# Two-layer spectral attention over 56 planes: the mix of images made once and kept, in three of four passes

## The chip, the cores and the metric

The kernel runs on one NeuronCore of a Trainium2 chip. Its five engines are TensorE (PE: matrix products; PEld stands for its weight loads), VectorE (DVE), ScalarE (ACT), GpSimd (POOL) and SyncE (SP, which issues the DMAs). The metric is the device time of one execution in microseconds, in fp32 throughout. A profile is one execution recorded by the hardware profiler; its span is the time from the first to the last recorded instruction.

## The reference

The input x holds 2 images (b = 0, 1), each of K = 56 planes of 128 x 128. Two layers follow each other, each of the form x = x + conv(gn(x)). Cut to what matters here:

```python
for layer in (0, 1):
    xa = gn(x)                               # one plane each: B*K planes of one channel
    q, k, v = (fno(inorm(xa)) for 3 sets)    # 1 channel -> 8 heads
    out  = softmax(q k^T / 128) v            # over the 56 planes, per head
    att  = inorm(fno_P(out) + xa)            # 8 heads -> 1 channel
    h    = gelu(inorm(spectral_M0(inorm(att))) + skip_M0(inorm(att)))
    h    = inorm(spectral_M1(h)) + skip_M1(h)
    x    = x + inorm(h) + att
```

Here `fno` is a spectral convolution (rfft2, a product on 2 x 16 x 16 modes, irfft2) plus a skip of 1 x 1. All skips are linear in the planes, so everything of `att` that is not confined to the few kept modes is one 56 x 56 matrix applied to the planes of the image: the "mix of images". It enters the forward path twice in a layer, each time times one factor per plane: once below the gelu, and once in the residual at the end.

## The kernel before, in words

One pass is one image in one layer; the kernel makes four: pass 0 and 1 are layer 0 with b = 0 and 1, pass 2 and 3 layer 1. The image stands in SBUF as X2 (partitions: 56 planes twice over, upper and lower rows of a chunk; row 56 of each half is a row of constants), and everything else of a pass happens in the space of modes. The stages of a pass and the names used for them are single letters, which are also tokens of the order of work:

- t (turn): PE transposes the image in 8 pieces, ACT copies them to P (L420); k: DVE's bn_stats of the planes (L426); m, n: forward transform; g, c: gram matrix of the modes for the norms.
- q (`scale_x`, L610): POOL multiplies X2 in place by the factor gvr of each row, in 8 pieces of 1024 columns; after the last a DMA puts gvr itself in row 56 of X2.
- u, s, v, a, d: scores, values, softmax and heads, from which the matrix BTx of the mix comes.
- p (`norms_chain`, from L773): the norms. From sums over the modes it makes three factors per plane, spread out as w; it transforms the low modes back halfway (`inverse`), and then makes two scaled copies of the matrix, Bs = BTx * w0 and Be = BTx * w2.
- y (`gelu`): for each of 8 slots of 1024 columns, PE puts the synthesis of the low modes in a PSUM pair (`synthesis`, L828, 16 matmuls for a slot), adds the mix of X2 with Bs (`mixed`, L843, 4 matmuls of 512 columns for a slot), and ACT takes the gelu of that PSUM pair to P (L859). `h3(b, n)` is slot n of P.
- z (`gelu_stats`, L866): DVE's bn_stats of the gelu's output, two for a slot. b (`turn_back`): PE transposes the slots (L409), ACT copies them out (L876). f (`forward`, L893): PE's transform back to modes. h (`h_chain`): the second spectral layer and its norms on these modes, ending in the factor hs (L957).
- x (`end_x`): loads of the residual x into xr, which has three slots of 1024 columns, by SP's DMAs; in pass 3 POOL restores it from X2 instead (`from_x2`, L981).
- e (`end_sums`): per slot again a synthesis, and again the mix of X2, now with Be; in pass 3 also xr, by a matmul (L1007).
- o (`end_out`): DVE makes h * hs + the PSUM pair (L1018), POOL adds xr (L1021, not in pass 3), and SP stores: to `out` in layer 1, to a DRAM buffer in pass 0. Layer 0 leaves the new x in X2.
- W, R, A, B, C, O prepare the weights, mostly on POOL.

The order of work is written out by hand as one string of tokens, ORDER: each token is a letter with the number of the pass, and advances that pass's generator by one step. Every engine executes its instructions in exactly this order (`_in_order`); between engines a tile framework sets the semaphores. So one instruction that has to wait holds back all that follow on its engine. PSUM has two rotating banks (`bank`) and three rotating pairs of banks (`pair`), given out in the order of the calls.

Of the kernel before, what the change touches and what calls it, by code (L numbers as in the profile page):

```python
# [37 lines left out]
F32 = mybir.dt.float32  # L38
# [105 lines left out]
t0 t0 t0 t0 W0 t0 t0 t0 x0 k0 k0 k0 k0 k0 k0 k0 t0 k0 m0 m0 m0 n0 m0 n0 m0 m0 W0 W0 W0 t1 W0 k1 n0 m0 m0 n0 n0 t1 t1  # L144
t1 g0 g0 g0 g0 k1 k1 k1 g0 R0 g0 n0 q0 q0 t1 t1 t1 t1 R0 R0 k1 k1 k1 R0 k1 m1 R0 A0 A0 A0 g0 g0 c0 c0 m1 u0 u0 m1 n1
m1 m1 n1 n1 c0 m1 n1 m1 n1 n1 u0 u0 u0 s0 g1 g1 g1 W1 W1 m1 g1 g1 g1 g1 g1 c1 A0 s0 s0 c1 u0 u0 u0 c1 u1 u1 W1 u1 s1
u1 u1 B0 B0 B0 s0 s0 x0 s1 s1 u1 u1 u1 s0 a0 s1 s1 v1 v0 v0 a0 v0 B0 s1 a1 v0 v0 a0 W1 W1 R1 d0 d0 d0 d0 a0 v1 a0 p0
v1 a1 q0 C0 p0 p0 p0 v1 v1 O0 p0 q0 q0 q0 q0 q0 a1 d1 d1 p0 p0 p0 a1 p0 d1 d1 q1 a1 p1 R1 q1 p1 p1 p1 y0 y0 z0 y0 R1
R1 R1 z0 b0 b0 p1 R1 y0 C0 R1 y0 y0 f0 f0 f0 b0 q1 q1 z0 z0 x0 q1 q1 q1 y0 y0 y0 p1 p1 b0 f0 b0 p1 p1 f0 b0 f0 z0 z0
y0 y0 y0 f0 f0 q1 b0 y1 f0 z0 z0 b0 y1 f0 f0 f0 y1 y1 y1 y1 b1 b1 h0 h0 h0 h0 h0 h0 z1 z1 y1 y1 y1 y1 z1 z1 z1 z1 y1  # L150
h0 f1 f1 f1 z1 y1 z1 b1 b1 h0 h0 f1 b1 f1 b1 f1 h0 f1 f1 b1 f1 h0 h0 b1 f1 f1 f1 h1 h0 e0 e0 o0 e0 x0 h1 o0 x0 e0 e0
t2 e0 e0 e0 o0 h1 h1 h1 h1 e0 e0 x0 o0 x0 e0 e0 o0 x0 t2 o0 o0 x1 k2 h1 k2 t2 o0 h1 h1 h1 k2 t2 k2 h1 t2 k2 h1 t2 t2
t2 e1 A1 h1 O1 e1 k2 k2 k2 x1 x1 e1 e1 e1 o1 x1 e1 o1 m2 o1 m2 e1 e1 e1 t3 t3 x1 o1 o1 x1 x1 x1 o1 k3 m2 m2 m2 m2 m2
t3 t3 k3 e1 e1 n2 n2 o1 x2 n2 n2 e1 o1 x2 t3 m2 t3 g2 g2 g2 g2 A1 A1 k3 k3 k3 k3 t3 t3 g2 g2 g2 g2 k3 c2 n2 n2 k3 m3
m3 c2 B1 C1 u2 u2 m3 n3 m3 m3 m3 m3 n3 n3 c2 u2 n3 n3 n3 q3 q3 u2 u2 m3 g3 g3 g3 g3 A1 g3 s2 g3 g3 g3 s3 s2 s2 c3 u2
u2 u2 u3 u3 u3 u3 c3 s2 s2 s2 B1 B1 B1 s3 s3 a2 v2 v2 u3 u3 u3 u3 a2 v2 v2 q2 q2 q2 a2 q2 q2 q2 q2 s3 s3 c3 C1 v2 s3
a3 d2 d2 d2 d2 a2 v3 a2 p2 a3 v3 p2 p2 p2 v3 v3 v3 p2 a3 d3 d3 q3 q3 q3 q3 p2 p2 p2 a3 p2 d3 d3 a3 y2 q2 y2 y2 p3 p3
p3 p3 b2 b2 p3 z2 f2 y2 y2 y2 p3 b2 f2 b2 z2 f2 p3 y2 y2 y2 z2 z2 p3 p3 f2 f2 b2 y2 b2 y2 y2 z2 z2 z2 z2 q3 f2 f2 f2
f2 q3 b2 y3 b2 y3 x2 z3 y3 z3 f2 f2 f2 b3 y3 b3 y3 y3 h2 h2 h2 h2 f3 f3 f3 y3 y3 y3 z3 h2 z3 z3 h2 b3 b3 h2 z3 f3 f3
f3 b3 b3 h2 h2 y3 y3 f3 h2 y3 b3 h2 h2 h2 f3 f3 b3 f3 f3 e2 e2 f3 e2 e2 e2 e2 e2 h3 o2 x2 o2 x2 o2 x2 h3 h3 h3 z3 o2  # L160
x2 z3 h3 e2 h3 h3 x3 e2 o2 x2 h3 h3 e2 e2 e2 o2 h3 o2 h3 h3 h3 x3 o2 x3 x3 e3 e3 o3 e3 e3 e3 x3 e3 x3 x3 x3 e3 e3 e3
e3 e3 o3 o3 x3 o3 o3 o3 o3 e3 o3
# [19 lines left out]
def fno_layers(ctx: ExitStack, tc: tile.TileContext, x, out, weights, small, const):  # L182
# [9 lines left out]
    ps = pool("psum", 2, space=bass.MemoryType.PSUM)  # L192
    pq = pool("pair", 3, space=bass.MemoryType.PSUM)
    dp = pool("dram", 1, space=bass.MemoryType.DRAM)

    def bank():
        return ps.tile([N, 512], F32, name="bank")

    def pair():
        return pq.tile([N, 2, 512], F32, name="pair")  # L200

    def little(name, shape):
        return sm.tile(shape, F32, name=name)
# [38 lines left out]
    V.memset(eps, EPS)  # L242
    ones = cp.tile([K, N], F32, name="ones")
# [16 lines left out]
    def padded(name, rows, m, n):  # L260
# [6 lines left out]
    xf_, gc_, BT_, Bs_, Be_ = (  # L267
        padded(*a) for a in (("xf", N, 448, 456), ("gc", K, K, 64), ("BT", K, K, 64), ("Bs", N, K, 64), ("Be", N, K, 64))
    )
# [336 lines left out]
    def scale_x(L, b):  # L606
        gvr = st[L][b]["gvr"]
        for o in range(0, 64, 8):
            v = X2[:120, b, o : o + 8, :]
            G.tensor_tensor(v, v, _bc(gvr[:120], 1, 8), ALU.mult)  # L610
            if o == 56:
                for c in range(2):
                    k = 64 * c + K
                    Q.dma_start(out=X2[k : k + 1, b], in_=_bc(gvr[k : k + 1, :], 1, 64))
            yield
# [157 lines left out]
    def norms_chain(L, b):  # L773
# [26 lines left out]
        V.reciprocal(k3, k3)  # L800
        yield
        w = rows([k3[:, 1:2], k3[:, 2:3], k3[:, 0:1]], [over[:, 1], over[:, 2], over[:, 0]])
        p = pair()
        t, dc, dq = p[:, 0, :448], p[0:1, 1, :K], p[0:1, 1, K : 2 * K]
# [12 lines left out]
        V.tensor_tensor(Bs_[b][:, :K], s["BTx"][:, :K], w[:, 0, :], ALU.mult)  # L817
        yield

        V.tensor_tensor(Be_[b][:, :K], s["BTx"][:, :K], w[:, 2, :], ALU.mult)  # L820
# [3 lines left out]
    def synthesis(A, both, Z):  # L824
        for e in range(4):
            for j in range(4):
                o = 64 * (8 * A + 2 * e)
                T.matmul(  # L828
                    both[j // 2][:, j % 2, N * e : N * e + N], lhsT=Z[32 * j : 32 * j + 32, o : o + N],
                    rhs=C["gw"][32 * j : 32 * j + 32, :], start=(e == 0), stop=False, tile_position=(32 * j, 0),  # L830
                    skip_group_check=True,
                )

    def mixed(L, b, A, v, p, Bs, stop=True):

        for c in range(2):
            s = 16 * A + (8 * v + 4 * c if L == 0 else 8 * c + 4 * v)  # L840
            for r in range(2):
                q = slice(64 * r, 64 * r + K + 1)
                T.matmul(  # L843
                    p[64 * c : 64 * c + 64, r, :], lhsT=Bs[q, :], rhs=X2[q, b, s : s + 4, :].rearrange("p e w -> p (e w)"),
                    start=False, stop=stop, tile_position=(64 * r, 64 * c), skip_group_check=True,
                )

    def h3(b, n):
        return P[b][:, 1024 * n : 1024 * n + 1024]

    def gelu(L, b):
        s = st[L][b]
        for A in range(4):
            both = [pair(), pair()]
            synthesis(A, both, s["Z"])
            yield
            for v in range(2):
                mixed(L, b, A, v, both[v], Bs_[b])
                S.activation(h3(b, 2 * A + v), both[v].rearrange("p r m -> p (r m)"), AF.Gelu)  # L859
                yield  # L860

    def gelu_stats(L, b):
        stats = st[L][b]["h"] = little(f"stats{b}", [N, 16, 6])
        for n in range(8):
            for r in range(2):
                V.bn_stats(stats[:, 2 * n + r, :], h3(b, n)[:, 512 * r : 512 * r + 512])  # L866
            yield
# [33 lines left out]
    def h_chain(L, b):  # L901
# [8 lines left out]
        V.bn_aggr(mv, s["h"].rearrange("p n s -> p (n s)"))  # L910
        V.tensor_scalar(mv[:, 1:2], mv[:, 0:1], mv[:, 0:1], mv[:, 1:2], ALU.mult, ALU.add)
        V.tensor_scalar(mv, mv, 0.5, None, ALU.mult)
# [80 lines left out]
    def end_sums(L, b):  # L993
        s = st[L][b]
        for A in range(4):
            both = [pair(), pair()]
            s["ends"] = s.get("ends", []) + both
            synthesis(A, both, half[b])
            yield
            for v in range(2):  # L1000
                n = 2 * A + v
                mixed(L, b, A, v, both[v], Be_[b], not from_x2(L, b))
                if from_x2(L, b):
                    for c in range(2):
                        for r in range(2):
                            q = slice(64 * r, 64 * r + K)
                            T.matmul(  # L1007
                                both[v][64 * c : 64 * c + 64, r, :], lhsT=C["fold"][q, :],
                                rhs=xr[q, n % 3, 512 * c : 512 * c + 512], start=False, stop=True,
                                tile_position=(64 * r, 64 * c), skip_group_check=True,  # L1010
                            )
                yield

    def end_out(L, b):
        s = st[L][b]
        for n in range(8):
            h, p = h3(b, n), s["ends"][n]
            V.scalar_tensor_tensor(h, h, s["hs"], p.rearrange("p r m -> p (r m)"), ALU.mult, ALU.add)  # L1018
            X, to = (X2[:, b, 8 * n : 8 * n + 8, :].rearrange("p e w -> p (e w)"), between[0]) if L == 0 else (h, far[1][b])
            if not from_x2(L, b):  # L1020
                G.tensor_tensor(X, h, xr[:, n % 3, :], ALU.add)  # L1021
            if L == 1 or b == 0:
                for c in range(2):
                    Q.dma_start(
                        out=to[0, c, :, n // 2, 2 * (n % 2) : 2 * (n % 2) + 2],
                        in_=X[64 * c : 64 * c + K].rearrange("p (r m) -> p r m", r=2),
                    )
            yield


    streams = {}
    for L in range(2):
# [6 lines left out]
        for b in range(B):  # L1039
            for name, stream in (  # L1040
                ("t", turn), ("k", count), ("m", modes_chain), ("n", normalise), ("g", gram), ("c", gram_chain),
                ("q", scale_x), ("u", u_x), ("s", scores), ("v", values), ("a", softmax_chain), ("d", heads),
                ("p", norms_chain), ("y", gelu), ("z", gelu_stats), ("b", turn_back), ("f", forward), ("h", h_chain),
# [58 lines left out]
```

## Time and profile before

| | us |
|---|---|
| median of 3 runs | 442.13 |
| lowest and highest run | 438.7, 443.82 |
| profiled execution | 436.31 |
| its span | 434.4 |
| PE busy in the span | 374.3 (86%) |
| DVE busy | 260.5 (60%) |
| POOL busy | 254.3 (59%) |
| ACT busy | 188.0 (43%) |
| mean granted clock of PE | 0.95 of full |

In lines of groups, the entries are: source line, engine, operation, tiles written <- tiles read, shape, count, then busy time in us and mean ns of one, then the idle time of the engine just before them and what ended most of it. In a table of windows each row is one stretch of the span, with the busy us of each engine in it and the number of instructions in brackets. In the chain that ended last each piece is one stretch of work of one engine, reached by going back from the last instruction to what released it. In a line of the timeline the first two numbers are start and length, and the square brackets hold the engine's idle time before it and what ended that. Of interest are two long pauses of POOL, 39.4 us up to 190.26 us (until DVE's first L1018 of pass 0) and 59.0 us from 323.3 us on, and ACT's idle time of some 246 us.

### The profile page before, as it was taken

What the parts mean: (1) busy time and instruction counts of PE and PEld (TensorE: products, weight loads), DVE (VectorE), ACT (ScalarE), POOL (GpSimd) and SP (SyncE); (2) the same over time, 40 slices, a digit from 0 to 9 for tenths busy, and PEclk for the clock granted to TensorE, in tenths of its full rate; (3) what the DMA queues carried; (4) which work ended last, traced back from release to release, by engine and by line L of the source; (5) the groups of instructions that cost most, each with busy time, mean ns of one, the idle gap of its engine ahead of it and who ended that gap; (6) DMA issues with size and microseconds to landing.
All of it is one profiled execution on the core that took longest, in us unless ns stands there. A gap on an engine that the chain in (4) does not pass through costs nothing.

```text
span 434.4 us, 15733 instructions
## 1 busy us (share of the span) xinstructions
PE 374.3 (86%) x7138; PEld 262.9 (61%) x7138; DVE 260.5 (60%) x456; ACT 188.0 (43%) x254; POOL 254.3 (59%) x263
## 2 busy tenths in 40 slices
PE   2457498999999999989689999999989999887894
PEld 1325485878985655745554677878857566535541
DVE  1548347013574879788778965024545987788553
ACT  2336046167616566612322635476546677503000
POOL 2059769999898800045919674998950000065893
PEclk9999789999999999999569999999996999999598
DMA  7999820000020010018736220000021000048465
GB/s 177 210 244 207 116 67 4 3 5 4 3 49 5 4 7 2 3 43 275 257 108 167 67 70 4 5 3 3 2 13 46 2 3 4 2 123 273 136 192 171
DMA packets 13171, 33.38 MB, mean 77 GB/s; under 512 B 2080, under 2 KB 2848, under 8 KB 13088
## 3 DMA queue, kind: packets, MB, share of 16 engines
q1 hardware_dynamic: 12960, 32.31, 28.8%
q8 instruction: 56, 0.92, 0.9%
q10 hardware_dynamic: 144, 0.07, 0.1%
q14 instruction: 11, 0.09, 0.1%
HBM read 21.09 MB, written 11.01 MB: 74 GB/s over the span
## 4 chain that ended last, share of the span: by engine, by line
PE 58%; DVE 15%; issue 13%; DMA 6%; POOL 4%; ACT 3%; SPq 0%; DVEq 0%; POOLq 0%; ACTq 0%
PE pair L843 8%; PE bank L570 8%; PE pair L828 5%; PE pair L409 5%; DMA X<-x 4%; PE pair L686 4%; POOL X L610 3%; PE pair L637 3%; DVE P L1018 3%; PE bank L664 3%; PE pair L453 3%; DVE WT L526 3%; PE pair L763 2%; PE bank L436 2%; PE pair L519 2%
## 5 line engine op out<-in xcount | busy, mean ns | idle before, releaser
L610 POOL TENSOR_TENSOR X<-X,gvr 120x1024 f32<-120x1024 f32 x32 | 74.6, 2357 | 11.7 <-ACT gvr L562 11.7
L1021 POOL TENSOR_TENSOR X<-P,xr 128x1024 f32<-128x1024 f32 x16 | 38.4, 2419 | 51.3 <-DVE P L1018 46.3
L1021 POOL TENSOR_TENSOR P<-P,xr 128x1024 f32<-128x1024 f32 x8 | 18.8, 2359 | 65.8 <-issue 59.0
L1018 DVE SCALAR_TENSOR_TENSOR P<-P,hs,pair 128x1024 f32<-128x1024 f32 x32 | 40.3, 1271 | 18.0 <-PE pair L1007 11.2
L426 DVE BATCH_NORM_STATS2 stats<-P 128x6 f32<-128x448 f32 x64 | 35.2, 610 | 26.0 <-ACT P L420 26.0
L420 ACT COPY P<-pair 128x896 f32<-128x896 f32 x32 | 27.9, 909 | 46.0 <-PE pair L409 46.0
L866 DVE BATCH_NORM_STATS2 stats<-P 128x6 f32<-128x512 f32 x64 | 39.6, 681 | 6.3 <-ACT P L859 6.3
L409 PE MATMUL pair<-C,X 56*128 56x56 f32 x512 | 26.4, 256 | 17.0 <-DMA X<-x 9.3
L570 PE MATMUL bank<-P 128*64 128x56 f32 (+1 forms) x1024 | 33.7, 230 | 6.6 <-issue 5.9
L409 PEld LDWEIGHTS pair<-C,X 56*128 56x128 f32 x512 | 23.1, 166 | 24.6 <-DMA X<-x 8.9
L570 PEld LDWEIGHTS bank<-P 128*64 128x64 f32 (+1 forms) x1024 | 32.9, 145 | 8.3 <-issue 7.3
L859 ACT ACTIVATE P<-pair 128x1024 f32<-128x1024 f32 x32 | 31.4, 1022 | 14.0 <-PE pair L843 12.1
L843 PE MATMUL pair<-X,Be 57*64 57x512 f32 x256 | 35.2, 648 | 0.0
L843 PE MATMUL pair<-X,Bs 57*64 57x512 f32 x256 | 33.0, 606 | 1.0 <-DMA X<-gvr 1.0
L876 ACT COPY WT<-pair 128x896 f32<-128x896 f32 x32 | 28.4, 908 | 11.8 <-PE pair L409 11.7
L828 PEld LDWEIGHTS pair<-C,WT 32*128 32x128 f32 x512 | 19.2, 204 | 13.1 <-DVE P L1018 5.4
L828 PE MATMUL pair<-C,WT 32*128 32x128 f32 x512 | 23.2, 305 | 3.5 <-DVE WT L458 2.0
L409 PEld LDWEIGHTS pair<-C,P 56*128 56x128 f32 x512 | 19.1, 143 | 10.4 <-issue 4.4
L409 PE MATMUL pair<-C,P 56*128 56x56 f32 x512 | 22.1, 232 | 1.2 <-DVE WU L948 0.5
L828 PE MATMUL pair<-C,P 32*128 32x128 f32 x512 | 20.1, 293 | 0.0
L519 PE MATMUL pair<-P,fwg 128*32 128x448 f32 x128 | 15.2, 595 | 5.3 <-ACT fwg L507 2.1
L828 PEld LDWEIGHTS pair<-C,P 32*128 32x128 f32 x512 | 16.9, 194 | 4.6 <-issue 3.1
(240 smaller groups left out, 760.9 us busy)
## 6 DMA issues: line engine op xcount, KB each, us to landing
X<-x SPq DMA_DIRECT2D x16, 448.0 KB
xr<-x SPq DMA_DIRECT2D x32, 224.0 KB
out<-P SPq DMA_DIRECT2D x32, 224.0 KB
store<-X SPq DMA_DIRECT2D x16, 224.0 KB
xr<-store SPq DMA_DIRECT2D x16, 224.0 KB
stage<-weights SPq DMA_DIRECT2D x2, 544.0 KB
C<-const_all SPq DMA_DIRECT2D x1, 808.5 KB
X<-x SPq DMA_DIRECT2D x2, 256.0 KB
```

The lines of the kernel that those rows point to most:

```text
L409: T.transpose(p[:, c, o : o + K], rows[q, :], ident[q, q], tile_position=(64 * c, 0))
L420: S.copy(dst.rearrange("p x c k -> p c x k"), p[:, :, :448].rearrange("p c (x k) -> p c x k", x=8))
L426: V.bn_stats(stats[:, n, :], P[b][:, 448 * n : 448 * n + 448])
L570: T.matmul(p[u : u + m, :K], lhsT=P[b][:, K * i : K * i + m], rhs=plane[b][:, i, :], start=(i < 2), stop=(i == N - 1), tile_position=(0, u ...
L610: G.tensor_tensor(v, v, _bc(gvr[:120], 1, 8), ALU.mult)
L828: T.matmul(both[j // 2][:, j % 2, N * e : N * e + N], lhsT=Z[32 * j : 32 * j + 32, o : o + N], rhs=C["gw"][32 * j : 32 * j + 32, :], start ...
L843: T.matmul(p[64 * c : 64 * c + 64, r, :], lhsT=Bs[q, :], rhs=X2[q, b, s : s + 4, :].rearrange("p e w -> p (e w)"), start=False, stop=stop, ...
L859: S.activation(h3(b, 2 * A + v), both[v].rearrange("p r m -> p (r m)"), AF.Gelu)
L866: V.bn_stats(stats[:, 2 * n + r, :], h3(b, n)[:, 512 * r : 512 * r + 512])
L876: S.copy(hT[n % 2].rearrange("p r e c k -> p c (r e) k"), p[:, :, :448].rearrange("p c (x k) -> p c x k", x=8),)
L1018: V.scalar_tensor_tensor(h, h, s["hs"], p.rearrange("p r m -> p (r m)"), ALU.mult, ALU.add)
L1021: G.tensor_tensor(X, h, xr[:, n % 3, :], ALU.add)
```

## The change

In passes 0, 1 and 2 the mix with the unscaled matrix BTx is computed once (new stream E, `mixes`) and copied by ACT from PSUM over the image in X2, which nobody reads after that. Everything that the mix was used for is then made from this copy:

- y makes only the synthesis on PE; DVE adds X2 times the factor qc0 to it and writes P. The gelu is a stream of its own, j, and reads P instead of PSUM (in pass 3 still PSUM). It also accumulates its sum over each slot.
- S (`scale_mixes`): ACT multiplies the slots of X2 in place by the factor qc1. i (`add_x`): POOL adds xr to them. e makes only the synthesis, and o adds the X2 slot where it added xr.
- z, in all four passes: ACT's Square of each slot with an accumulated sum, in place of DVE's bn_stats; h then reduces two sums instead of aggregating bn_stats.
- The two scaled matrices are made in pass 3 alone; p makes the factors qc with two small multiplications, one small matmul and a copy.
- Three streams of tiny activations (lx, ls, lg) stand in ORDER to place loads of ACT's function tables. By the order of activations there are 19 table loads, before 16.
- PSUM banks and pairs are fixed tiles now, given out by two strings, BANKS and PAIRS. ORDER has 809 tokens instead of 713 and is another order throughout.

```diff
-a3 d2 d2 d2 d2 a2 v3 a2 p2 a3 v3 p2 p2 p2 v3 v3 v3 p2 a3 d3 d3 q3 q3 q3 q3 p2 p2 p2 a3 p2 d3 d3 a3 y2 q2 y2 y2 p3 p3
+p2 E2 x2 E2 p2 E2 p2 p2 a3 E2 E2 v3 p2 y2 y2 y2 lg j2 z2 q3 q3 q3 q3 S2 a3 j2 y2 y2 y2 j2 q3 d3 S2 d3 S2 y2 y2 y2 a3
...
+    banks = [ps.tile([N, 512], F32, name=f"bank{n}") for n in range(2)]
+    pairs = [ps.tile([N, 2, 512], F32, name=f"pair{n}") for n in range(3)]
...
     def pair():
-        return pq.tile([N, 2, 512], F32, name="pair")
+        return pairs[int(next(next_pair))]
...
+        if not from_x2(L, b):
+            f2 = little(f"f2{b}", [K, 2])
+            V.tensor_scalar(f2[:, 0:1], k3[:, 1:2], d["A0m0"][:K], None, ALU.mult)
+            V.tensor_scalar(f2[:, 1:2], k3[:, 0:1], par["gan"][:K], None, ALU.mult)
...
+        if not from_x2(L, b):
+            T.matmul(p[:, 1, 128:130], lhsT=C["dup"][:K, :], rhs=f2, start=True, stop=True)
+            qc = s["qc"] = little(f"qc{b}", [N, 2])
+            V.tensor_copy(qc, p[:, 1, 128:130])
...
+    def slots(L, b, n):
+        if L == 0:
+            return X2[:, b, 8 * n : 8 * n + 8, :].rearrange("p (r e) w -> p r (e w)", r=2)
+        x8 = X2[:, b, 16 * (n // 2) : 16 * (n // 2) + 16, :]
+        return x8.rearrange("p (c v s) w -> p v c (s w)", c=2, v=2)[:, n % 2]
+
+    def pieces(L):
+        return [slice(0, 2)] if L == 0 else [slice(0, 1), slice(1, 2)]
...
+    def mixes(L, b):
+        for n in range(0 if from_x2(L, b) else 8):
+            E = pair()
+            mixed(L, b, n // 2, n % 2, E, st[L][b]["BTx"], True)
+            for r in pieces(L):
+                S.copy(slots(L, b, n)[:, r], E[:, r])
+            yield
...
             for v in range(2):
-                mixed(L, b, A, v, both[v], Bs_[b])
-                S.activation(h3(b, 2 * A + v), both[v].rearrange("p r m -> p (r m)"), AF.Gelu)
+                n = 2 * A + v
+                if from_x2(L, b):
+                    mixed(L, b, A, v, both[v], Bs)
+                else:
+                    V.scalar_tensor_tensor(
+                        h3(b, n).rearrange("p (r m) -> p r m", r=2), slots(L, b, n), s["qc"][:, 0:1], both[v], ALU.mult, ALU.add,
+                    )
...
+            S.activation(h3(b, n), src, AF.Gelu, accum_out=sums_[:, 0, n : n + 1])
...
+    def scale_mixes(L, b):
+        for n in range(0 if from_x2(L, b) else 8):
+            for r in pieces(L):
+                t = slots(L, b, n)[:, r]
+                S.activation(t, t, AF.Copy, scale=st[L][b]["qc"][:, 1:2])
+            yield
+
+    def add_x(L, b):
...
+                xs = xr[:, n % 3, :].rearrange("p (r m) -> p r m", r=2)[:, r]
+                G.tensor_tensor(t, t, xs, ALU.add)
...
-            for r in range(2):
-                V.bn_stats(stats[:, 2 * n + r, :], h3(b, n)[:, 512 * r : 512 * r + 512])
+            S.activation(stage[:, :1024], h3(b, n), AF.Square, accum_out=st[L][b]["h"][:, 1, n : n + 1])
...
-        V.bn_aggr(mv, s["h"].rearrange("p n s -> p (n s)"))
-        V.tensor_scalar(mv[:, 1:2], mv[:, 0:1], mv[:, 0:1], mv[:, 1:2], ALU.mult, ALU.add)
-        V.tensor_scalar(mv, mv, 0.5, None, ALU.mult)
+        V.tensor_reduce(mv, s["h"], AX.X, ALU.add)
+        V.tensor_scalar(mv, mv, 1.0 / (N * N), None, ALU.mult)
...
-            synthesis(A, both, half[b])
+            synthesis(A, both, half[b], not from_x2(L, b))
...
             if not from_x2(L, b):
-                G.tensor_tensor(X, h, xr[:, n % 3, :], ALU.add)
+                G.tensor_tensor(X, hv, x2, ALU.add)
...
+    def tables(func, n):
+        for _ in range(n):
+            S.activation(tiny, eps[0:1], func)
+            yield
```

## The prediction

> **What bounds the kernel now.** I read first the busy time of each engine in the whole span, then the chain that ended last, then the costliest groups, and last a table of windows cut at the places where a pass changes stage.
>
> ```profile
> PE 374.3 (86%) x7138; PEld 262.9 (61%) x7138; DVE 260.5 (60%) x456; ACT 188.0 (43%) x254; POOL 254.3 (59%) x263
> PE 58%; DVE 15%; issue 13%; DMA 6%; POOL 4%; ACT 3%; SPq 0%; DVEq 0%; POOLq 0%; ACTq 0%
> ```
>
> TensorE is busy for 86% of the span and holds 58% of the chain; ScalarE is the emptiest engine. An average cannot say whether a stage has room, so here are the windows. The columns are start and end, length, then busy time of PE, PEld, DVE, ACT and POOL, the granted clock, DMA share and GB/s. The cuts are: first gelu of pass 0 (133.0), the factor hs of pass 1 ready (223.4), first gelu of pass 2 (323.0), last turned-back copy of pass 3 (378.3).
>
> ```profile
> 0.00:133.00 133.00, 101.39 (x2226) 80.95 (x2227) 56.95 (x113) 55.48 (x77) 98.41 (x168) 0.97 0.41 89
> 133.00:223.40 90.40, 81.94 (x1300) 53.24 (x1302) 73.55 (x124) 43.36 (x58) 39.05 (x25) 0.93 0.29 84
> 223.40:323.00 99.60, 93.85 (x2193) 70.48 (x2195) 53.79 (x96) 47.09 (x67) 78.69 (x52) 0.98 0.15 36
> 323.00:378.30 55.30, 52.83 (x877) 34.50 (x873) 39.81 (x76) 38.24 (x47) 0.56 (x2) 0.94 0.06 12
> 378.30:434.40 56.10, 44.30 (x554) 23.70 (x554) 36.44 (x48) 3.78 (x8) 37.58 (x17) 0.89 0.57 173
> ```
>
> The second and fourth windows hold the gelu stages. PE is 91% and 96% busy in them, ACT 48% and 69%. In the fourth, the chain shows the beat, start and length in us:
>
> ```profile
> 343.10 1.10 PE pair L828 x32
> 344.20 0.65 PE pair L409 x16
> 344.86 1.88 PE pair L843 x16
> 346.73 0.89 PE bank L893 x16
> 347.63 0.64 PE pair L409 x16
> 348.26 1.10 PE pair L828 x32
> ```
>
> One beat (two slots of 1024 columns) takes 5.16 us: 1.10 synthesis, 1.88 mix, 0.89 forward, 1.29 transposes. The mix costs 0.235 us a matmul. The rows that price the rest:
>
> ```profile
> L859 ACT ACTIVATE P<-pair 128x1024 f32<-128x1024 f32 x32 | 31.4, 1022 | 14.0 <-PE pair L843 12.1
> L866 DVE BATCH_NORM_STATS2 stats<-P 128x6 f32<-128x512 f32 x64 | 39.6, 681 | 6.3 <-ACT P L859 6.3
> L1018 DVE SCALAR_TENSOR_TENSOR P<-P,hs,pair 128x1024 f32<-128x1024 f32 x32 | 40.3, 1271 | 18.0 <-PE pair L1007 11.2
> L610 POOL TENSOR_TENSOR X<-X,gvr 120x1024 f32<-120x1024 f32 x32 | 74.6, 2357 | 11.7 <-ACT gvr L562 11.7
> L876 ACT COPY WT<-pair 128x896 f32<-128x896 f32 x32 | 28.4, 908 | 11.8 <-PE pair L409 11.7
> L843 PE MATMUL pair<-X,Be 57*64 57x512 f32 x256 | 35.2, 648 | 0.0
> ```
>
> Three single instructions are needed below: two gelus back to back, the first gelu of pass 3, and the smallest ACT copy.
>
> ```profile
> 133.17 1.94 ACT L859 ACTIVATE P<-pair 128x1024 f32<-128x1024 f32 x2
> 346.00 1.94 ACT L859 ACTIVATE P<-pair 128x1024 f32<-128x1024 f32 x2
> 376.15 0.16 ACT L957 COPY hs<-bank 128x1 f32<-128x1 f32 x1 [0.57 <-PE bank L955]
> ```
>
> **What the Trainium skill says.** "ScalarE: Activation LUTs", section "What ACT_TABLE_LOAD costs", gives 186 ns plus 0.833 ns an element, some 93 ns of overlap between neighbours, and about 1283 ns a table load. The trace agrees: 1.02 us for 1024 elements, 1.94 us for two in a row, 1.28 us for the load before 133.17. That page prices no accumulator output; "VectorE: DVE Perf Modes", section "Two Vector instructions with no wait between them", says that on DVE such an output makes a second instruction. No row here shows one on ACT. "SBUF — State Buffer", section "Who interferes with whom", says that DVE instructions with at most one SBUF input do not hold GpSimd up; L1018, with one input in PSUM, is such a form, and so is the new one (slots in SBUF, synthesis in PSUM).
>
> **The change part by part.**
>
> *Mix once (PE).* In three passes the second mix (8 slots of 4 matmuls) goes: 96 x 0.235 = 22.6 us off PE. Its own busy row gives 3/4 of 35.2 = 26.4. I take 22.6, the rate on the chain.
>
> *Copies out (E, ACT).* The mix lands in X2 by 8 copies of 1024, or 16 of 512, a pass. By L859's duration: 24 x 1.02 = 24.5 us. *Scaling (S, ACT)*, in place: 24.5 us. *Squares (z, ACT)* for the second moment, all four passes: 32 x 1.02 = 32.6 us. Together +82 us; with three more table loads (19 for 16, 3.8 us) and 16 tiny activations of about 0.2 us, ACT goes from 188 to some 275 to 280 us.
>
> *Accumulators.* 64 ACT instructions now have one. Unknown: 0 if free, 0.16 to 0.20 each if it is a second small instruction (the smallest copy above). I take 0.15, 10 us in all, of which 5 in the stage of passes 0 and 1. A gain is excluded, since the instruction does no less than before.
>
> *DVE.* bn_stats goes (-39.6), 24 scalar_tensor_tensors of 1.27 come (+30.5), a few small ones come: about -8. *POOL.* 24 adds i at L610's 2.36: +57 us, to 311. The adds o are as many as before. In the second window POOL is 43% busy, waiting 39.4 us for the first o of pass 0: most of i lies there, at no cost so long as xr slots come in time. Exposed, one add is 2.4 us per slot. *SP's queue:* as many xr loads, but each waits for its slot (three of them) to be freed by i instead of o; behind a waiting load stand the stores of o, which are awaited only by the xr loads of pass 2 and by the end, so this costs nothing unless i is late.
>
> *Banks and small work.* Fixed banks and pairs replace rotation: no instruction, and a later reuse is hidden by PE's other streams; exposed, one wait is a gelu, 1 us. The two muls, the matmul and the copy for qc: some 0.6 us a pass, beside the inverse in p.
>
> *By stage, from sums of durations in the new order.*
> 1. To the first gelu: PE's ordered work comes to 84.1 us against 90.6 (relay and p1 moved behind; five E0 mixes in front). At the same idle share: -6, first gelu at 127.
> 2. Gelu stage of passes 0 and 1, to hs of pass 1 (90.4 us before). PE's sum falls to about 73, DVE's is 74, POOL's 78. ACT: 43.4 busy, plus 11 E, 15 S and 16 Squares (42 x 1.02 = 42.8), plus about 9 that move in (eight turn copies of pass 2 are 7.3) = 95.5. Less 0.1 for each of some 67 neighbours (6.7), plus 5 for accumulators: 93.6 us. So ACT alone fills more than the whole former stage. It cannot run without gaps: a square waits for its gelu, the gelu for DVE, DVE for the synthesis, h's two table loads sit between gelus of another pass, and all in fixed order. Before, PE led with 91%; I give ACT 89%: 93.6/0.89 = 105. That is +14.6, hs of pass 1 at 232 (+8.6).
> 3. To the first gelu of pass 2. PE's ordered work is 83.4 against 88.9 us, at the old ratio of elapsed to busy 88 us; and the 4.7 us for which the trace has the chain waiting on gvr's transfer into X2 are covered, because scale_x and mixes come earlier. First gelu at 324, 92 us instead of 99.6: -7.
> 4. First gelu of pass 2 to that of pass 3: 22.9 us before (346.0 - 323.1). ACT's ordered sum is now 30.8, about 28.5 back to back, plus accumulators and gaps: 32. +9.
> 5. From there to the last turned-back copy: 32.3 us before; ACT's 29 us of ordered work and DVE's lost bn_stats allow 30. -2. Then h3 to the end: eight squares (8 x 0.93) stand ahead of h3's first ACT step, about where bn_stats ended before; POOL's adds of pass 3 stay, and the end is PE's 2.35 us a slot in both. -2, for e2 without its mix.
> Sum: -6 +14.6 -7 +9 -2 -2 = +6.6, rounded to +6. The profiled execution took 436.3 (434.4 and 1.9 around it), so about 442.3, a factor of 1.014; on the median of 442.13 that is 448. That median lies 1.3% above the profiled execution, which bears on the range.
>
> **The rivals.**
> - *ACT takes the work in its gaps (faster).* For it: ACT idles 246 us; PE is 58% of the chain and loses 22.6; in step 2 everything sums to less than 96. If ACT fills the stage (91 us back to back with free accumulators) and step 4 costs 28 for 23: -6 +0.6 -7 +5 -2 -2 = -11, time 431. With half of the gaps: 438. Against: the gelu stages are just where ACT has least room (69% busy in the fourth window). Chance 0.22.
> - *ACT and the three pairs lock into each other (much slower).* A pair is held by synthesis until DVE has read it, by E until ACT has copied it; PE waits on a pair that waits behind a square. At 80% ACT use and 0.2 an accumulator, step 2 costs 95/0.80 = 119 (+28) and step 4 costs 36 (+13): -6 +28 -7 +13 -2 -2 = +24, time 466 at the worst; half-way 456. It decides from the point where ACT is below about 85%. Chance 0.20, in the slow side.
> - *POOL's adds end up late.* The i adds must precede o in each slot and pass 1's stand before the q's of pass 2. Sum on POOL from hs of pass 0 (197) to the last q2: 97 us, so 294, before the 310 at which mixes of pass 2 begin. Covered; if not, 5 us: 453. Chance 0.05.
> - *It cancels.* PE saves 22.6 but gets stalled as much; within 1%. Chance 0.18.
>
> **How the numbers follow.** The forecast (445 to 453) has 0.35, lock-up 0.20, POOL 0.05, cancel 0.18, gain 0.22. Slower by over 1%: 0.60; within 1% (about what a measurement of this kernel can tell from no change, whose runs span 1.2%): 0.18; faster by over 1%: 0.22. The range leaves out the better half of the gain (below 433) and the worst of the lock-up (above 460).
>
> **What would show it.** Step 1: the first gelu (ACT, P<-P) at 125 to 129. Step 2: ACT over 85% busy from there to hs of pass 1, PE below 80%, hs of pass 1 after 228; PE's idle put down to ACT. Step 3: no wait on gvr's transfer in front of the mixes of pass 2. Step 4: gelus of pass 3 some 32 us behind those of pass 2, ACT near full. Accumulators: a row of small ACT instructions beside gelu and square, or a mean above 1.02. It is wrong if ACT stays below 75% in step 2 and hs of pass 1 comes before 222: then PE's cut was worth its face value. It is wrong the other way if PE stands waiting for pairs while ACT too is idle.

## The result and the profile after

The changed kernel takes 456.98 us (median of 4 runs, 452.89 to 459.91) against 441.62 us before (median of 4): a ratio of 1.032, 95% interval 1.022 to 1.042 (the ratios here and below leave out executions that took over 1.5% longer than the fastest of their kernel; the medians keep them). It is slower. The profiled execution took 452.89 us with a span of 451.1 (before: 436.31 and 434.4).

The page of the changed kernel, busy time of the engines and shares of the chain that ended last:

```profile
PE 374.9 (83%) x6952; PEld 266.7 (59%) x6952; DVE 253.1 (56%) x415; ACT 279.7 (62%) x433; POOL 308.9 (68%) x294
PE 55%; DVE 13%; ACT 13%; DMA 10%; issue 4%; POOL 3%; SPq 0%; ACTq 0%; DVEq 0%
```

The work went where it was meant to go: ScalarE up from 188.0 to 279.7 us, GpSimd from 254.3 to 308.9. But TensorE is as long busy as before, with 186 matmul records less (a matmul of fp32 leaves two records here, so this is 96 matmuls of the second mix less and the three small ones for qc more). The costliest groups concerned, of the same kernel:

```profile
L871 PE MATMUL pair<-X,BTx 57*64 57x512 f32 x192 | 26.1, 616 | 0.3 <-issue 0.2
L939 POOL TENSOR_TENSOR X<-X,xr 128x1024 f32<-128x1024 f32 (+1 forms) x32 | 57.6, 1821 | 66.8 <-ACT X L930 59.9
L913 DVE SCALAR_TENSOR_TENSOR P<-X,qc,pair 128x1024 f32<-128x1024 f32 x24 | 29.9, 1271 | 11.4 <-PE pair L856 8.1
L944 ACT ACTIVATE stage<-P 128x1024 f32<-128x1024 f32 x32 | 33.8, 1057 | 0.5
L944 ACT ACTIVATION_READ_ACCUMULATOR stage<-P 128x1 f32 x32 | 6.1, 190 | 0.0
```

The mix takes 26.1 us in three passes, and 9.4 + 7.8 in the last: 43.3 in place of 33.0 + 35.2 = 68.2. So 24.9 us of matmuls are gone, and TensorE's busy time did not fall. The windows, cut at the same marks (first gelu of pass 0 at 126.4, hs of pass 1 at 234.4, first gelu of pass 2 at 333.1, last turned-back copy at 397.1; columns as before):

```profile
0.00:126.40 126.40, 98.46 (x2054) 74.38 (x2058) 57.71 (x107) 62.17 (x92) 91.01 (x146) 0.97 0.41 93
126.40:234.40 108.00, 88.76 (x1380) 62.41 (x1380) 74.02 (x117) 93.23 (x142) 77.67 (x57) 0.84 0.33 92
234.40:333.10 98.70, 90.58 (x2022) 65.96 (x2022) 54.27 (x93) 55.31 (x82) 74.26 (x53) 0.96 0.07 17
333.10:397.10 64.00, 59.62 (x1040) 42.81 (x1042) 34.93 (x61) 55.06 (x95) 23.66 (x19) 0.87 0.14 39
397.10:451.10 54.00, 37.45 (x472) 21.10 (x467) 32.23 (x40) 13.88 (x27) 42.32 (x21) 0.83 0.46 137
```

What changed most is the third column from the right, the granted clock of TensorE. It fell in the gelu stages from 0.93 to 0.84 and from 0.94 to 0.87, and at the end from 0.89 to 0.83. The line of the page that shows it in 40 slices, before:

```profile
PEclk9999789999999999999569999999996999999598
```

and after:

```profile
PEclk9999699999999799698856999999999599688699
```

From windows of 1 us each, TensorE's span can be split in three: idle time; busy time times the missing part of the clock, called lost (an estimate); and the rest, work at full clock.

| stage | length before, after | idle | lost | work |
|---|---|---|---|---|
| to the first gelu | 133.2, 126.4 | 32, 28 | 3, 2 | 98, 96 |
| gelu of passes 0 and 1 to hs of pass 1 | 90.2, 107.8 | 8, 19 | 5, 13 | 77, 76 |
| to the first gelu of pass 2 | 99.7, 98.9 | 6, 8 | 2, 3 | 92, 87 |
| to the first gelu of pass 3 | 22.9, 34.5 | 1, 4 | 3, 4 | 18, 27 |
| to the last turned-back copy | 32.3, 29.5 | 1, 0 | 0, 3 | 31, 25 |
| to the end | 56.1, 54.0 | 12, 16 | 4, 6 | 40, 32 |
| whole span | 434.4, 451.1 | 60, 76 | 17, 32 | 357, 343 |

Work fell by 15 us; idle time rose by 16 and lost time by 15. That sum is the 16.7 us of the span. The work fell by 10 us less than the rows of the mix, and which matmuls took those 10 us longer is not worked out here. The idle time of the second stage is in pieces of up to 3.2 us. The three longest in the timeline of TensorE after, idle time before the instruction in brackets:

```profile
212.53 2.08 PE L856 MATMUL pair<-C,WT 32*128 32x128 f32 x28 [3.23 <-ACT P L436]
227.50 1.10 PE L499 MATMUL bank<-over,f 56*128 56x56 f32 x4 [3.21 <-DVE f L1019]
230.65 3.36 PE L469 MATMUL pair<-WU,C 64*128 64x224 f32 x16 [2.05 <-DVE WU L1027]
```

Two of these lie in h of pass 1, the chain of small steps that ends in hs. By the waits of the whole stage, 12.0 us of TensorE's 19 us idle ended on an instruction of VectorE and 7.0 us on one of ScalarE; before, it was 7.3 and 0.7 us of 8.5.

### The profile page after: what moved, and what is told of

Its sections match the earlier page's. It is cut to its first block, busy times and chain, and to the rows that moved or that the text cites. A ratio compares the mean times of both kernels' runs of the same rounds, so it can differ in the third digit from the quotient of the medians.

```text
span 451.1 us, 15595 instructions
## 1 busy us (share of the span) xinstructions
PE 374.9 (83%) x6952; PEld 266.7 (59%) x6952; DVE 253.1 (56%) x415; ACT 279.7 (62%) x433; POOL 308.9 (68%) x294
## 4 chain that ended last, share of the span: by engine, by line
PE 55%; DVE 13%; ACT 13%; DMA 10%; issue 4%; POOL 3%; SPq 0%; ACTq 0%; DVEq 0%
PE pair L871 7%; DMA X<-x 7%; PE pair L856 7%; PE bank L586 5%; PE pair L781 4%; PE pair L425 4%; DMA stage<-weights 3%; PE pair L704 3%; ACT stage L944 3%; PE pair L655 3%; PE pair L469 3%; PE bank L682 3%; PE bank L971 3%; DVE P L913 2%; PE pair L535 2%
## 5 line engine op out<-in xcount | busy, mean ns | idle before, releaser
L939 POOL TENSOR_TENSOR X<-X,xr 128x1024 f32<-128x1024 f32 (+1 forms) x32 | 57.6, 1821 | 66.8 <-ACT X L930 59.9
L436 ACT COPY P<-pair 128x896 f32<-128x896 f32 x32 | 27.9, 903 | 24.4 <-PE pair L425 24.2
L1100 POOL TENSOR_TENSOR X<-P,X 128x1024 f32<-128x1024 f32 x16 | 37.5, 2382 | 6.1 <-DVE P L1095 6.1
L913 DVE SCALAR_TENSOR_TENSOR P<-X,qc,pair 128x1024 f32<-128x1024 f32 x24 | 29.9, 1271 | 11.4 <-PE pair L856 8.1
L944 ACT ACTIVATE stage<-P 128x1024 f32<-128x1024 f32 x32 | 33.8, 1057 | 0.5
L930 ACT ACTIVATE X<-X,qc 128x1024 f32<-128x1024 f32 (+1 forms) x32 | 28.3, 933 | 0.0
L896 ACT COPY X<-pair 128x1024 f32<-128x1024 f32 (+1 forms) x32 | 24.3, 802 | 6.3 <-PE pair L871 5.3
L662 ACT COPY P<-pair 128x896 f32<-128x896 f32 x16 | 14.5, 906 | 22.1 <-PE pair L655 21.9
L425 PE MATMUL pair<-C,P 56*128 56x56 f32 x512 | 25.0, 251 | 2.3 <-ACT P L923 1.1
L871 PE MATMUL pair<-X,BTx 57*64 57x512 f32 x192 | 26.1, 616 | 0.3 <-issue 0.2
L856 PE MATMUL pair<-C,P 32*128 32x128 f32 x512 | 23.4, 296 | 3.1 <-DVE P L913 1.2
```

What stands on the lines that cost most here:

```text
L425: T.transpose(p[:, c, o : o + K], rows[q, :], ident[q, q], tile_position=(64 * c, 0))
L856: T.matmul(both[j // 2][:, j % 2, N * e : N * e + N], lhsT=Z[32 * j : 32 * j + 32, o : o + N], rhs=C["gw"][32 * j : 32 * j + 32, :], start ...
L871: T.matmul(p[64 * c : 64 * c + 64, r, :], lhsT=Bs[q, :], rhs=X2[q, b, s : s + 4, :].rearrange("p e w -> p (e w)"), start=start, stop=stop, ...
L913: V.scalar_tensor_tensor(h3(b, n).rearrange("p (r m) -> p r m", r=2), slots(L, b, n), s["qc"][:, 0:1], both[v], ALU.mult, ALU.add,)
L930: S.activation(t, t, AF.Copy, scale=st[L][b]["qc"][:, 1:2])
L939: G.tensor_tensor(t, t, xs, ALU.add)
```

## The experiments

Each kernel is compared with the kernel before, run beside it; that one's median was 439 to 440 us here, against 441.6 beside the changed kernel. The changed kernel was not run again, so a difference from its 456.98 us is good to some 4 us (the 95% interval of its ratio is 1% either way). The theories at the start: A, ScalarE's added work is the bound of the gelu stages, as predicted; B, TensorE's half clock is the loss; C, GpSimd's adds delay the next layer.

**Without the accumulated sums.**

```diff
-            S.activation(h3(b, n), src, AF.Gelu, accum_out=sums_[:, 0, n : n + 1])
+            S.activation(h3(b, n), src, AF.Gelu)
-            S.activation(stage[:, :1024], h3(b, n), AF.Square, accum_out=st[L][b]["h"][:, 1, n : n + 1])
+            S.activation(stage[:, :1024], h3(b, n), AF.Square)
```

> The changed kernel without the accumulated sums of gelu and square, so the second layer's statistics are left out (a constant stands for them); everything else is executed. It takes 64 accumulator reads of 0.19 us, 12.3 us, off ScalarE, half of them in the gelu stage of passes 0 and 1. Theory A, ScalarE's added work is the bound of both gelu stages: step 2 shorter by about 6 us, step 4 by 2, in all 6 to 9 us less than the changed kernel (448 to 451). Theory B, the loss is TensorE's time at half its clock after gaps that come from chains of waits, whatever ScalarE's length: 0 to 3 us less (454 to 457).

Measured: 456.62 us, as the changed kernel (456.98). The accumulator reads cost 0.19 us each, 12.3 in all, as the trace shows them; taking them away gained nothing that can be seen. That is against A (448 to 451) and inside B's range.

**Statistics back on VectorE.**

```diff
-            S.activation(stage[:, :1024], h3(b, n), AF.Square, accum_out=st[L][b]["h"][:, 1, n : n + 1])
+            for r in range(2):
+                V.bn_stats(stats[:, 2 * n + r, :], h3(b, n)[:, 512 * r : 512 * r + 512])
```

> The changed kernel with the statistics of the gelu back on VectorE (bn_stats, 64 x 0.68 us), so squares and accumulator reads go: ScalarE loses 33.8 + 12.3 = 46 us, VectorE gains 43 us. Theory A: in step 2 ScalarE falls from 93 to about 71 us and VectorE rises from 74 to about 95, so step 2 falls from 108 to some 97; step 4 falls by 4; 10 to 15 us less than the changed kernel (442 to 447). Theory B: the chains of waits stay, 0 to 4 us less (453 to 457). If VectorE becomes the bound in turn: no gain or a loss.

Measured: 483.65 us, ratio to before 1.098 (1.091 to 1.106): 27 us more than the changed kernel. The second window of this run:

```profile
131.40:251.70 120.30, 96.36 (x1379) 67.67 (x1379) 92.84 (x151) 75.30 (x94) 74.16 (x45) 0.76 0.30 82
```

ScalarE fell from 93 to 75 us there and VectorE rose to 93, as expected; but the stage became 12 us longer, with the clock at 0.76. Both numbers failed. The loss is the third case of the expectation, VectorE as the bound in turn, so this run alone does not rule A out; it does show what work on VectorE costs. Over the whole span TensorE has 89 us idle and 50 lost, against 76 and 32.

**Scaling and x in one VectorE instruction.**

```diff
-                S.activation(t, t, AF.Copy, scale=st[L][b]["qc"][:, 1:2])
+                pass
-                G.tensor_tensor(t, t, xs, ALU.add)
+                V.scalar_tensor_tensor(t, t, st[L][b]["qc"][:, 1:2], xs, ALU.mult, ALU.add)
```

> The changed kernel with scaling of the kept mix (ScalarE, 28 us) and adding of x (GpSimd, 58 us) done by one VectorE instruction per piece in the place of the add (24 slots of about 1.3 us, 32 us). Theory A: ScalarE loses 15 of its 93 us in step 2, 6 to 10 us less there, some 8 to 12 us less in all (445 to 449). Theory C, GpSimd's adds between the last scaling of pass 1 and the turn of pass 3 take back the gain of step 3: in addition 3 to 6 us less in step 3 (439 to 446). Theory B: 0 to 4 us less.

Measured: 487.92 us, ratio 1.110 (1.102 to 1.118), 31 us more, though 28 us of ScalarE's and 58 of GpSimd's work became 35 of VectorE's. None of the three theories had a loss. One row seems to show a price that I had wrong:

```profile
L939 DVE SCALAR_TENSOR_TENSOR X<-X,qc,xr 128x1024 f32<-128x1024 f32 x16 | 24.4, 1532 | 1.9 <-DMA xr<-x 1.9
```

That is 1.53 us with both inputs in SBUF, against 1.27 for L913 with one in PSUM. But the mean hides two cases, of which the timeline shows one each:

```profile
200.23 1.27 DVE L939 SCALAR_TENSOR_TENSOR X<-X,qc,xr 128x1024 f32<-128x1024 f32 x1
209.03 2.69 DVE L939 SCALAR_TENSOR_TENSOR X<-X,qc,xr 128x1024 f32<-128x1024 f32 x1
```

Twelve of the 16 began while GpSimd was idle and took 1.22 to 1.28 us. The four that began while GpSimd was at work, as with L1100 at 209.03, took 1.47 to 2.72 us. The Trainium skill, "SBUF — State Buffer", section "Who interferes with whom", says that a VectorE instruction with two SBUF inputs contends with a GpSimd instruction that reads SBUF; the trace agrees. So the price of 1.3 us was right, and the waiting for GpSimd, some 4 us in all, is far short of the 31.

**Extra matmuls to hold the clock.** (One of three places is shown.)

```diff
+    def warm(p, n):
+        for _ in range(n):
+            T.matmul(p, lhsT=ident, rhs=Ct[:, : p.shape[-1]], start=True, stop=True, skip_group_check=True)
...
         sums(p, 0, s1, False, True)
+        warm(p[:, 16:], {0: 1, 1: 2, 2: 1, 3: 2}.get(2 * L + b, 0))
```

> The changed kernel with extra matmuls into unused columns of PSUM (some 0.9 us each at full clock), one to two after the column sums of the norm chains of passes 0 to 3 and two before the inverse of the second layer in passes 1 and 3: only the gaps of TensorE are filled, nothing else is changed. Theory B: about half of the eleven stretches at half clock go, the mean granted clock rises from 0.91 to about 0.94 and the time falls by 6 to 12 us (445 to 451). Theory A: the clock may rise but ScalarE holds the stages: within 2 us of the changed kernel, or longer by the extra work.

Measured: 462.47 us, ratio 1.048 (1.039 to 1.057), 5 us more. The twelve matmuls cost more than the 0.9 us that I had reckoned for each:

```profile
L499 PE MATMUL bank<-C 128*128 128x496 f32 x16 | 9.7, 711 | 0.0
L499 PE MATMUL pair<-C 128*128 128x512 f32 x8 | 6.7, 983 | 0.0
```

These two rows are the twelve matmuls, 16.4 us in all. B's range (445 to 451) failed; A's "longer by the extra work" fits. The mean clock rose to 0.923, but the lost time by the split above stayed at 32 us: the half clock moved to other places. Where the matmuls filled the gaps of pass 1 (hs of pass 0 to hs of pass 1) the stage took 39.8 us against 38.9. So filling the gaps in this way gains nothing; whether the clock could be held without extra work was not tried.

After these four runs I formed theory D: VectorE's instructions stand in the chain of every slot, and that is what counts.

**VectorE's addition below the gelu cut short.**

```diff
-                        h3(b, n).rearrange("p (r m) -> p r m", r=2), slots(L, b, n), s["qc"][:, 0:1], both[v], ALU.mult, ALU.add,
+                        h3(b, n).rearrange("p (r m) -> p r m", r=2)[:, :, :64], slots(L, b, n)[:, :, :64], s["qc"][:, 0:1], both[v][:, :, :64], ALU.mult, ALU.add,
```

> The changed kernel with VectorE's addition of the kept mix below the gelu cut to 64 of 512 columns, so that 7/8 of that addition is left out; every hand-over between engines stays. VectorE loses about 24 x 1.07 = 26 us, none of it on ScalarE or GpSimd. Theory D, formed after the first four runs (12 us off ScalarE gained nothing, 32 to 43 us put on VectorE cost 27 to 31): VectorE's instructions stand in the chain of every slot and are what the gelu stages follow: 12 to 25 us less than the changed kernel (432 to 445). Theory A, ScalarE bounds the stages: 0 to 4 us less (453 to 457).

Measured: 457.08 us, the same as the changed kernel. D (432 to 445) fell too: making VectorE's instructions shorter gains nothing, though adding to VectorE's work cost 27 and 31 us.

**No scaling and no x.**

```diff
-                S.activation(t, t, AF.Copy, scale=st[L][b]["qc"][:, 1:2])
+                pass
-                G.tensor_tensor(t, t, xs, ALU.add)
+                pass
```

> The changed kernel with the scaling of the kept mix on ScalarE (28 us) and the adding of x on GpSimd (58 us) both left out, so the residual is left out; loads of x stay. Theory A or C: ScalarE's and GpSimd's sums count: 8 to 15 us less than the changed kernel (442 to 449). Theory D: 0 to 5 us less, because VectorE's work is the same (452 to 457).

Measured: 455.75 us, 1.2 less than the changed kernel, for 86 us of work on two engines. A and C (442 to 449) are both out, and the number lies in D's range, though D had fallen: the add on GpSimd, which stands on the chain at 252.6 to 255.0 us, is replaced by something as late when it goes.

**The old order with the mix made once.** The tokens E, j, S, i put in the old ORDER by rule:

```diff
-y0 y0 z0 y0 ...
+E0 E0 y0 y0 j0 z0 S0 i0 y0 j0 ...
```

> Mix made once and kept, as in the changed kernel, in the order of the kernel before: mixes in front of each synthesis of the gelu stage, gelu behind each addition, scaling behind each square, the add of x where x has come; no tiny activations; pairs of PSUM banks given out by longest free. If the new order is what costs: 430 to 445. If the reuse itself costs (longer chain of a slot, VectorE and ScalarE in the gelu stages): 455 to 480.

Measured: 627.73 us, far outside both. Two waits of this run point to the reason (us in total, times, longest):

```profile
POOL X L940 <- DMA xr<-x: 38.7, 7, 6.3
POOL X L940 <- ACT X L931: 34.9, 5, 12.0
```

My rule put the add right behind the load of x, so GpSimd stands for 74 us in these two, and what is behind it too; that this makes the whole of the 170 us is not shown. Moreover the squares' scratch buffer still holds weights of layer 1 in this order, so these are overwritten. It does not tell order from reuse.

**The new order with the mix made twice.**

```diff
-                    V.scalar_tensor_tensor(
-                        h3(b, n).rearrange("p (r m) -> p r m", r=2), slots(L, b, n), s["qc"][:, 0:1], both[v], ALU.mult, ALU.add,
-                    )
+                mixed(L, b, A, v, both[v], Bs_[b])
+                if not from_x2(L, b):
+                    one_gelu(L, b, n)
...
-                G.tensor_tensor(X, hv, x2, ALU.add)
+                G.tensor_tensor(X, hv, xr[:, n % 3, :].rearrange("p (r m) -> p r m", r=2), ALU.add)
```

> The order of the changed kernel with the mix made twice by TensorE, as before: no copies, no scaling, no add of x to the mix, no addition on VectorE below the gelu; gelu from PSUM at the place of that addition; squares stay on ScalarE. The residual is added from the loaded slots in this order, so some slots get another piece of x (that part of the output is wrong, the work is the same). TensorE gets 22.6 us back. If the new order is what costs: 452 to 470. If the reuse itself costs: 436 to 446.

Measured: 500.08 us, ratio 1.136 (1.128 to 1.145), 43 us above the changed kernel where 22.6 us of matmuls came back. By the numbers it points to the order, but the run before shows that a mismatch between an order and its work can cost far more than this; I don't take it as proof of either.

The last four runs put two theories against each other. F: what is left is TensorE's own order with its gaps and its half clock, and matmuls that are removed turn into gaps. G: several chains of nearly equal length run beside each other, so that relieving one shows nothing.

**All relieved at once.** The edits of the first, fifth and sixth run together, and squares of 64 columns.

```diff
-            S.activation(stage[:, :1024], h3(b, n), AF.Square, accum_out=st[L][b]["h"][:, 1, n : n + 1])
+            S.activation(stage[:, :64], h3(b, n)[:, :64], AF.Square)
```

> The changed kernel with everything relieved at once that was taken away one by one before: no accumulated sums, squares of 64 of 1024 columns only, VectorE's addition below the gelu cut to an eighth, no scaling, no adding of x (statistics, most of the mix below the gelu and the residual are left out). ScalarE loses some 70 us, VectorE 26, GpSimd 58; TensorE's work and every hand-over but those of the scaling and the add stay. Theory G, several chains of nearly the same length run beside each other, so that relieving one gained nothing: 425 to 440. Theory F, what is left is TensorE's own order, its gaps in the short chains of the second layer and its half clock: 448 to 457.

Measured: 451.97 us, ratio 1.028 (1.020 to 1.037). Its second window:

```profile
128.20:232.60 104.40, 84.24 (x1356) 58.05 (x1350) 60.11 (x117) 63.44 (x95) 44.10 (x40) 0.87 0.34 98
```

ScalarE is down by 30 us in this stage, VectorE by 14, GpSimd by 34, and the stage is 3.6 us shorter. TensorE's idle and lost time in the whole span are 74 and 36 us, against 76 and 32. So the lengths of the added instructions make up 5 of the 15 us at most: by the medians it is 5.0, by the ratios to the kernel before 1.6, by the profiled spans 0.9. The number is in F's range, and G (425 to 440) fell. One added length stayed: the copies E (L896), 24.4 us of ScalarE, each of which holds a PSUM pair until it is done.

**The second mix put back, on constants.**

```diff
-            synthesis(A, both, half[b], not from_x2(L, b))
+            synthesis(A, both, half[b])
+            for v in range(0 if from_x2(L, b) else 2):
...
+                        T.matmul(
+                            both[v][64 * c : 64 * c + 64, r, :], lhsT=s["BTx"][q, :], rhs=Ct[q, 512 * c : 512 * c + 512],
```

> The changed kernel with the matmuls of the second mix put back in their place in the ends of passes 0 to 2, on constants in place of the image (so that they wait for nothing, and the output is not the reference's); 22.6 us of TensorE's time come back, nothing else changes. Theory F, these matmuls stood in gaps of TensorE: 0 to 8 us more than the changed kernel (457 to 465), with a higher granted clock. Theory G: 15 to 25 us more (472 to 482).

Measured: 473.05 us, 16 more (19 by the ratios). This is in G's range (472 to 482), and F's number failed: idle and lost time stayed at 77 and 32 us and work rose from 343 to 364. In the new order these matmuls fill no gap, and leaving them out is worth most of their 22.6 us.

**The kernel before without the second mix.**

```diff
-                mixed(L, b, A, v, both[v], Be_[b], not from_x2(L, b))
                 if from_x2(L, b):
+                    mixed(L, b, A, v, both[v], Be_[b], False)
```

> The kernel before without the second mix in passes 0 to 2 (that part of the residual is left out), in its own order, with no other change: what the saving of TensorE's 22.6 us is worth by itself. Theory F: 2 to 9 us less than before (431 to 438). Theory G: 16 to 22 us less (418 to 424).

Measured: 434.23 us, ratio 0.987 (0.983 to 0.990): 5.9 us for 22.6 us of matmuls, in F's range. Its second window:

```profile
137.20:226.60 89.40, 79.94 (x1238) 54.97 (x1234) 72.92 (x123) 43.31 (x57) 39.08 (x25) 0.85 0.28 84
```

Against 90.40 us and a clock of 0.93 before. In the whole span, work fell by 24 us; idle time rose from 60 to 72 and lost time from 17 to 30. The profiled execution was one of the longer ones (437.87 us), so these two are somewhat high; but the lower clock is in all 20 executions, 0.884 to 0.927, against 0.929 to 0.955 in the 23 of the kernel before.

**The kernel before without the first mix.**

```diff
-                mixed(L, b, A, v, both[v], Bs_[b])
+                if from_x2(L, b):
+                    mixed(L, b, A, v, both[v], Bs_[b])
```

> The kernel before without the first mix, the one below the gelu, in passes 0 to 2 (left out), in its own order: the same 22.6 us of matmuls at another place, in the gelu stages where TensorE was over 90% busy. Theory F, the place decides: 14 to 22 us less than before (418 to 426), clearly more than the run without the second mix. Theory G: as much as the run without the second mix.

Measured: 429.07 us, ratio 0.974 (0.966 to 0.983): 11 us, more than without the second mix, as F had it, but short of F's 14 to 22; G had the same gain for both. The second window of this run:

```profile
132.60:223.90 91.30, 79.33 (x1188) 56.40 (x1189) 72.61 (x123) 43.11 (x56) 39.26 (x26) 0.82 0.27 83
```

The stage in which TensorE had been 91% busy lost the matmuls of 16 slots and became no shorter (90.4 before). The gain came later: 95.2 us against 99.7 to the first gelu of pass 2, and 52.5 against 55.3 in the window after it. In the whole span work fell by 22 us, idle time rose by 7, lost time by 8.

## Why the prediction was right in sign and size, and wrong in its reason

The forecast was 448 us, slower, with a range of 433 to 460; measured were 457. By its own steps:

1. *To the first gelu, -6:* measured -6.8 (126.4 us). Right.
2. *Gelu stage of passes 0 and 1, +14.6:* measured +17.5. The quantities were near (ScalarE 93.2 us busy, 86% of the stage; VectorE 74.0; GpSimd 77.7; TensorE 82%, where I had below 80), and the reason was wrong, so that the length came out near is luck. I read that ScalarE's sum fills the stage and so sets its length. With ScalarE at 63 us in the run with all relieved, the stage still took 104.4. This step failed. In its place the traces show 11 us more idle time and 8.5 us more lost clock on TensorE, with the same work in the stage (76 against 77). The sign that I had named, TensorE's idle time put down to ScalarE, did not come: that is 7 of 19 us.
3. *To the first gelu of pass 2, -7:* measured -0.8. TensorE's work fell by 5 us as summed, but 2 us of gaps and 1 us of lost clock came, and the wait for gvr's transfer was covered only to be followed by a chain through ScalarE's scaling and five adds of GpSimd (252.6 to 264.3 us). Leaving out the add of x, one of the five, did not shorten the stage either (100.3 us). This is the largest error of a size, 6 of the 10 us between forecast and measurement.
4. *To the first gelu of pass 3, +9:* measured +11.6.
5. *-2 and -2 for the rest:* measured -2.8 and -2.1.

*TensorE, -22.6:* its own row fell by 24.9. *ScalarE:* 279.7 us against 275 to 280. *Accumulators, 0.15 each with bounds of 0 and 0.20:* 0.19, a second instruction indeed, and worth nothing in time. *VectorE -8:* -7.4. *GpSimd 311:* 308.9.

A term that the prediction put at nothing is the growth of TensorE's gaps and half clock when matmuls go. The two runs on the kernel before show it without any of the additions: 22.6 us of matmuls less bring 5.9 or 11 us, the rest comes back as gaps and as half clock. It depends on the order: in the new one, the same matmuls put back cost 16 us. The faster rival also left this term out. The rival of a lock-up between ScalarE and the pairs had the nearest number (456 half-way) but its mechanism is not shown: relieving ScalarE of some 30 us in the stage did not free TensorE, though the copies E, which hold the pairs, kept their length in that run.

Put side by side, the runs give 440 us for the kernel before, 434 for it without the second mix, 452 for the changed kernel with all added lengths but E's cut, and 457 for the changed kernel. So the saving alone is worth 6 us, and some 18 us come on top that are not the lengths that were cut. The gaps and the half clock are not peculiar to the new order: the old order already has 72 us idle and 30 lost without the second mix, and 67 and 25 without the first, against 76 and 32 in the changed kernel. What differs between the changed kernel and the old order without the second mix is mostly the column of work, 333 against 343.

What stays open is the cause of those 18 us. It may lie in the copies E, in the hand-overs of E, gelu and square, or in the new order itself. Neither of the two runs that crossed order and reuse separates these, the one run of the new order without E's copies made the mix twice, and the hand-overs taken away with the order kept were only those of the scaling and the add.

## What to carry to other kernels

Split the bounding engine's time into work, gaps and lost clock before crediting a saving, and price the saving by leaving the work out of the old kernel: one run, here 5.9 us for 22.6. The price holds for that place in that order. Where an order is fixed by hand, the sum of an engine's work in a stage is not a length of the stage even at 86%: shorten that engine's work alone, and if nothing moves, it was not the bound. Work moved onto an engine that seems to have room may cost two thirds of its length or more (27 and 31 us for 43 and 35 us on VectorE), while taking 26 us off the same engine gained nothing.

## What the runs showed of the hardware

The clock fell without a pause. Three windows of the changed kernel, 2 us each:

```profile
380.00:382.00 2.00, 2.00 (x58) 1.82 (x54) 1.11 (x2) 1.70 (x6) 0.00 (x0) 1.00 0.03 8
382.00:384.00 2.00, 1.90 (x42) 1.77 (x39) 0.98 (x3) 2.00 (x4) 0.00 (x0) 1.00 0.00 0
386.00:388.00 2.00, 2.00 (x30) 2.00 (x26) 1.24 (x6) 1.70 (x3) 0.00 (x0) 0.50 0.00 0
```

TensorE is shown 95 to 100% busy from 380 us on, and the clock is at 0.50 from 384.9 to 391.8. The timeline of TensorE shows most of what ran in the 3.4 us before it fell, with 0.1 us idle between the two:

```profile
381.13 1.20 PE L425 MATMUL pair<-C,P 56*128 56x56 f32 x32
382.57 1.79 PE L504 MATMUL bank<-C,WU 128*56 128x1 f32 x32
```

These are transposes, and column sums of one column a matmul. The Trainium skill, "TensorE: Matmul & The Clock Gate", section "What's actually happening", has the array at half rate by default, released by activity in windows of some 3.4 us. The traces agree in the length: every stretch at half clock that the end of the span does not cut off is a multiple of 3.4 us, in the changed kernel 3.4, 6.8 or 10.2, and so in the traces of all fourteen kernels. That section names an idle window as the cause; here windows that the profile shows as busy were followed by half clock. The fourteen traces have 25 such falls, with TensorE shown at least 94% busy in the 3.4 us before. All 25 have one-column sums in these 3.4 us, 1.2 to 2.2 us of them. Transposes are in 16 only, so they are not needed for it. One without, in the run with extra matmuls, at 321.28 us, as the window before it and two pieces of its timeline:

```profile
317.87:321.28 3.41, 3.30 (x72) 2.64 (x64) 2.38 (x4) 3.10 (x5) 2.02 (x8) 1.00 0.00 0
318.51 1.14 PE L490 MATMUL pair<-P,WM 64*64 64x56 f32 x32
319.75 1.94 PE L510 MATMUL bank<-C,P 128*56 128x1 f32 x32
```

That the sums do not count as activity is not shown by this: no run changed them, and of 101 bursts of such sums that began at full clock, 55 saw a fall during them or within 3.4 us of their end.

An accumulated output of ScalarE is a second instruction of 0.19 us (64 of them, 12.3 us), near the upper bound of 0.20 that I had taken from the smallest copy.
